# Four source blocks in one weight tile, and a new order list, in a four-layer graph network on one Trainium2 core

## The chip, the core and the metric

The kernel runs on one core of a Trainium2 chip. A core has engines that run side by side, each working through its own queue of instructions in the order in which they were written into it: TensorE for matrix products (PE in the profile; PEld is its weight load), VectorE (DVE), ScalarE (ACT), GpSimd (POOL) and SyncE (SP, which here only starts transfers). They wait for one another through semaphores. The metric is the device time of one execution in microseconds; lower is better. The time before is the median of 3 runs.

## What is computed

Sixteen graphs of 1024 nodes with 256 features each pass through four layers. Every layer normalises, applies relu, runs a graph layer and adds the result to its input. All four use the same 0/1 adjacency of their graph.

```python
h = relu(layernorm(x))
# layer 0: neighbours' mean of h @ W_msg, plus h @ W_upd + bias, relu
x = x + relu(h @ W_upd + (adj.T @ (h @ W_msg)) / deg + bias)
# layers 1 and 2: attention of 4 heads of 64 features
w = h @ W                                   # per head
alpha = softmax(where(adj, leaky(e_src[:, None] + e_dst[None, :]), -1e9))
# layer 1: relu(alpha @ w + bias) + w, layer-normed per head;  layer 2: elu(alpha @ w)
# layer 3: attention with one head of 256 features
x = x + alpha @ (h @ W3.T)
```

`adj` is 16 x 1024 x 1024, `x` is 16 x 1024 x 256, all products in float32.

## The kernel before

**Attention without a softmax pass.** The kernel uses that exp(leaky(s + d)) is a product of an exponential of each end, times the larger of two terms. For one block of 128 source nodes (`jb`, 8 blocks) one DVE instruction in `masked` (L1085) computes max(row, column) times the mask for all target nodes of a stretch. The result, a tile `p`, is the stationary operand of the products on PE. The products also sum the weights in an added column, so that dividing by it ends the softmax.

**Layers 1 and 2** (`heads`, L1235): for each of 4 heads, eight `masked` calls of 1024 targets each, and for each an 0.94 us group of products (L1266) into one accumulator `acc` in PSUM, of which there are two. `weighted` (L1285, L1286) then divides and so frees the accumulator; an epilogue follows (`epilogue1` or `epilogue2`), whose result `added` (L1218, L1229) puts on `x`: the first three heads by a transfer that accumulates, the fourth by the DVE.

**Layer 3** (`layer3`, L1396): four strips (`i2`) of 256 targets. For each strip, eight `masked` calls of 256 targets, each into a `p` tile of its own that could hold 1024 columns; for each call two float32 products, which the trace shows as four records (L1420). Then a reciprocal (L1434) and two instructions that divide and add `x` (L1445), and the transfer of the result.

**Layer 0** (`layer0`, L1094) is mostly PE work: the projection is split into two float32r parts, and the sums over neighbours (L1145, L1148) read the adjacency, which POOL's queue fetches (L884). Each layer begins with `norm_t` (L913): statistics on the DVE (L927, L934), a power on POOL (L939, L940), a shift (L946), ACT (L959), transposes on PE (L972), a copy by ACT (L978). `terms` (L1014) prepares the exponentials, checks their bounds (L1059, L1060) and sends the rows through DRAM; `spread` fetches a row `r` to all partitions (L1069).

**The order is made by a list scheduler, in Python, while the kernel is built.** Each `do(engine, cost, fn, r, w, ...)` adds an operation to a `Plan`, with an assumed cost in microseconds, the buffers that it reads and writes, and a priority (smaller is more urgent). The priority is `plan.pos` (the PE cost of all that stands before it in its graph, plus the graph's offset `b * SHIFT`, 81.5), plus a `slack`, plus a number from the table `RANK` by stage and engine. `emit` (L115) repeatedly takes the operation that could start first by its assumed times; among equals, the smaller priority. The result is a fixed order on each engine. On the chip only the true dependencies, tile by tile, hold; the assumed times do not.

**Buffers.** A tile is made when its first operation is taken from the list. `BUFS` says how many of a kind may live at once: `p` 6, `r` 3, `mask` 3, `x` 3, `acc` 2, `mm` 4. The `p` tiles are shared by all three attention layers and by the graphs in work. In the list, graph b + 2 begins after layer 3 of graph b has begun (`gates`), so two graphs are interleaved, and for a while a part of a third.

Lines spoken of: `SHIFT` L28, `RANK` L31, `do` L85, `emit` L115, `bounds` L1058, `masked` L1079, `heads` L1235, `root` L1338, `layer3` L1396, the loop over graphs L1470.

Of the kernel before, what the change touches and what calls it, by code (L numbers as in the profile page):

```python
# [19 lines left out]
P = 128  # L20
# [6 lines left out]

SHIFT = 81.5  # L28

ENGINES = ("pe", "dve", "act", "pool", "sp")  # L30
RANK = {  # L31
    "load": (-164, -252, -233, -49, -101),
    "setup": (62, -81, -47, -39, -40),
    "norm0": (-115, -341, -486, -366, -276),
    "split0": (-189, -171, -200, -288, -222),
    "mask": (426, 519, 210, 415, 404),
    "gather0": (17, -41, 92, -16, -30),
    "norm1": (-244, -92, -259, -207, -131),
    "project1": (81, 8, 5, -19, -5),
    "weights1": (-184, 20, 105, 30, 9),  # L40
    "heads1": (-93, -221, -225, -190, -118),
    "last1": (77, -76, 54, -54, 59),
    "norm2": (-121, 40, 113, 26, 32),
    "project2": (60, -110, 135, 69, 0),
    "weights2": (-27, 12, 158, -73, -4),
    "heads2": (50, -14, -243, -121, -62),
    "last2": (-122, -176, -355, -98, -89),
    "norm3": (-9, -93, -182, -62, -63),
    "project3": (301, 122, 43, 220, 174),
    "weights3": (273, 71, 138, -93, 118),  # L50
    "last3": (58, 3, 157, 80, 48),
}
# [20 lines left out]
class Plan:  # L73
# [8 lines left out]
    def __init__(self):  # L82
        self.ops, self.pos, self.gate, self.stage = [], 0.0, None, None

    def do(self, eng, cost, fn, r=(), w=(), lag=0.0, slack=0.0, kind="f", dma=0.0):  # L85

# [22 lines left out]
        bufs = list(dict.fromkeys(key[0] if isinstance(key, tuple) else key for key in (*r, *w)))  # L109
        deps.discard(k)  # L110
        self.ops.append((eng, cost, lag, fn, deps, bufs, self.pos + slack + RANK[self.stage][ENGINES.index(eng)], kind, dma))
        if eng == "pe":
            self.pos += cost

    def emit(self):  # L115
# [14 lines left out]
        while ready:  # L130
            best = None
            for k in ready:
# [9 lines left out]
                for buf in bufs:  # L142
                    if buf.t is None:
# [3 lines left out]
                        if len(ends) >= m:  # L147
# [3 lines left out]
                            at = max(at, ends[m - 1] + 0.1)  # L151
                if at is not None and (best is None or (at, prio, k) < best):
                    best = (at, prio, k)
            at, _, k = best
            eng, cost, lag, fn, deps, bufs, _, kind, dma = self.ops[k]
# [444 lines left out]
def tile_factored(  # L600
# [413 lines left out]
    def terms(wh, xw, nh, slope, ecol, scol, k):  # L1014
# [46 lines left out]

        do("dve", 0.3, bounds, r=[et, (xw, "ed")], slack=12.0)

# [14 lines left out]

    def masked(r, tt, mask, jb, h, lo, hi):  # L1079

        w = buf(work, "p", [P, N])
        do(
            "dve",
            (hi - lo + 125) / 960.0,
            lambda: nc.vector.scalar_tensor_tensor(  # L1085
                w.t[:, : hi - lo], r.t[:, lo:hi], tt.t[:, 1, h, jb : jb + 1], mask.t[:, jb, lo:hi], op0=ALU.max, op1=ALU.mult
            ),
            r=[r, (tt, 1), mask],
            w=[w],
        )  # L1090
        return w
# [143 lines left out]
    def heads(b, l, xs, mask, w, slope, epilogue, keep):  # L1235
# [15 lines left out]
        for h in range(H):  # L1251
# [23 lines left out]
            plan.stage = f"heads{l}" if h + 1 < H else f"last{l}"  # L1275
            epilogue(b, h, ps, wh, xs, 11.0 if h + 1 < H else 0.0)

# [18 lines left out]
    def epilogue1(b, h, ps, wh, xs, slack):  # L1296
# [44 lines left out]

        do("pool", 2.0, root, r=[mb], w=[rs], lag=0.9, slack=slack)
        do(
# [52 lines left out]
    def layer3(b, xs, mask):  # L1396
# [15 lines left out]
        for i2 in range(NB // 2):  # L1412
            plan.stage = "weights3"
            ps = buf(acc_p, "acc", [P, 2, 512])
            for jb in range(NB):
                w = masked(r, tt, mask, jb, 0, i2 * 2 * P, (i2 + 1) * 2 * P)

                def product(w=w, ps=ps, jb=jb):
                    for q in range(2):
                        nc.tensor.matmul(  # L1420
                            ps.t[:, q, : D + 1],
                            w.t[:, q * P : (q + 1) * P],
                            wh.t[:, jb, : D + 1],
                            start=(jb == 0),
                            stop=(jb == NB - 1),
                        )

                do("pe", 0.87, product, r=[w, (wh, jb)], w=[ps])
            k = b * NB + 2 * i2
# [11 lines left out]
            for q in range(2):  # L1441
                do(
                    "dve",
                    0.5,
                    lambda q=q, i2=i2, ps=ps, o=o, k=k: nc.vector.scalar_tensor_tensor(  # L1445
                        o.t[:, q, :],
                        ps.t[:, q, :D],
                        rdn[:, k + q : k + q + 1],
                        xs.t[:, 2 * i2 + q, :],
                        op0=ALU.mult,  # L1450
                        op1=ALU.add,
                    ),
                    r=[ps, xs],
                    w=[(o, q)],
                )
# [15 lines left out]
    for b in range(B):  # L1471
        plan.pos, plan.gate = b * SHIFT, gates.get(b)
        xs, adjr = load_x(b) if b else first, {k: load_adjr(b, k) for k in range(2)}
        mask = buf(graph, "mask", [P, NB, N], U8)
        layer0(b, xs, adjr, mask)
        heads(b, 1, xs, mask, w1c, 0.01, epilogue1, True)
        heads(b, 2, xs, mask, w2c, 0.2, epilogue2, False)
        gates[b + 2] = len(plan.ops)
        layer3(b, xs, mask)
# [76 lines left out]
```

## The time and the profile before

| | us |
|---|---|
| runs | 2736.37, 2742.13, 2742.22 |
| median | 2742.13 |
| profiled execution, its own time | 2752.51 |
| its span, first to last instruction | 2750.2 |

The profile is one execution. Busy time counts an engine's instructions, not its waits; a busy PE counts matmuls that overlap and those at a lower clock. The 40 slices each cover 68.8 us; a digit is tenths of the slice, 9 is 90% or more:

```profile
PE   7877999999999999999999999999999999999786
DVE  2699499797979979799897978979799797979984
ACT  4651745554554545545554553555545554554232
PEclk9989999999999999999999999999999999999998
```

In the middle the picture repeats every 160 to 170 us, one graph's share: slices where the DVE is at 9 (head layers) and slices where it is at 7 (layers 0 and 3). At both ends PE is at 6 to 8.

### The profile page before, as it was taken

The page shows a single profiled execution, that of the slowest core. Times are in us where ns is not written, and L with a number is a line of the kernel's source. Part 1 is how long each engine was busy: PE and PEld are TensorE (multiplying, and loading weights), DVE is VectorE, ACT ScalarE, POOL GpSimd, SP SyncE. Part 2 cuts the span into 40 slices and gives each one's busy share as a digit, 9 for nine tenths or more (in the row PEclk, how much of TensorE's full clock was granted, in tenths as well). Part 3 has the DMA queues.
Part 4 walks back from the last instruction along what each step waited for, and adds up shares of the span by engine and source line. Part 5 has one row for each costly group of instructions (what it writes and reads, how often), then busy time and mean ns, then how long its engine had stood idle before and what let it go on. Part 6 is the DMA issues. An engine that isn't in the chain of part 4 may idle for free.

```text
span 2750.2 us, 93332 instructions
## 1 busy us (share of the span) xinstructions
PE 2539.9 (92%) x40667; PEld 2265.3 (82%) x40667; DVE 2280.5 (83%) x4646; ACT 1382.1 (50%) x3777; POOL 851.7 (31%) x913
## 2 busy tenths in 40 slices
PE   7877999999999999999999999999999999999786
PEld 6766889888888888888888888888888888888675
DVE  2699499797979979799897978979799797979984
ACT  4651745554554545545554553555545554554232
POOL 3332324224242422424133242422415133241210
PEclk9989999999999999999999999999999999999998
DMA  9724647265674726556273654826657284663221
GB/s 196 172 45 92 132 89 162 51 158 84 130 111 83 165 61 140 105 117 125 57 168 72 135 102 84 163 59 139 106 101 141 48 172 76 133 101 82 34 53 28
DMA packets 397325, 293.64 MB, mean 107 GB/s; under 512 B 179301, under 2 KB 345706, under 8 KB 396906
## 3 DMA queue, kind: packets, MB, share of 16 engines
q0 software_dynamic: 232992, 92.29, 27.8%
q1 hardware_dynamic: 160752, 193.05, 24.7%
q8 instruction: 321, 5.26, 0.8%
q10 hardware_dynamic: 3162, 2.24, 0.3%
q14 instruction: 98, 0.80, 0.1%
HBM read 228.21 MB, written 17.37 MB: 89 GB/s over the span
## 4 chain that ended last, share of the span: by engine, by line
PE 39%; DVE 29%; issue 9%; POOL 8%; ACT 4%; DMA 3%; SPq 0%; POOLq 0%; DVEq 0%; ACTq 0%
DVE p L1085 12%; PE mm L989 10%; PE acc L1266 10%; PE acc L1420 9%; DVE st L927 4%; POOL rsh L1340 3%; PE mm L1184 3%; PE mm L972 3%; ACT t L1356 3%; DVE t L1369 2%; DMA x<-y 2%; DVE sth L1329 2%; DVE t L1286 2%; POOL rsh L1339 2%; DVE t L1318 1%
## 5 line engine op out<-in xcount | busy, mean ns | idle before, releaser
L1085 DVE SCALAR_TENSOR_TENSOR p<-r,et,mask 128x1024 f32<-128x1024 f32 (+1 forms) x1536 | 1471.1, 1010 | 239.2 <-PE acc L1420 179.4
L1266 PE MATMUL acc<-wide,p 128*64 128x65 f32 x32768 | 1042.8, 225 | 107.8 <-DVE p L1085 55.1
L1266 PEld LDWEIGHTS acc<-wide,p 128*64 128x64 f32 x32768 | 1001.0, 140 | 171.6 <-issue 87.8
L1420 PE MATMUL acc<-wide,p 128*128 128x257 f32 x2048 | 490.7, 394 | 59.2 <-DVE p L1085 57.9
L1420 PEld LDWEIGHTS acc<-wide,p 128*128 128x128 f32 x2048 | 393.5, 196 | 131.0 <-DVE p L1085 63.6
L989 PE MATMUL mm<-f_w,ht 128*128 128x264 f32 (+2 forms) x2048 | 476.9, 385 | 1.3 <-ACT ht L978 0.6
L989 PEld LDWEIGHTS mm<-f_w,ht 128*128 128x128 f32 x2048 | 380.2, 191 | 60.1 <-ACT ht L978 6.2
L959 ACT ACTIVATE hn<-x,shift,rstd 128x256 f32<-128x256 f32 x512 | 272.1, 592 | 239.4 <-DVE shift L946 185.7
L939 POOL TENSOR_SCALAR rstd<-mv 128x4 f32<-128x4 f32 x128 | 52.2, 407 | 763.8 <-DVE mv L934 623.9
L1356 ACT ACTIVATE t<-t,mh,rsh 128x64 f32<-128x64 f32 x512 | 176.5, 428 | 185.9 <-DVE mh L1346 161.8
L978 ACT COPY ht<-mm 128x512 f32<-128x512 f32 x256 | 144.1, 578 | 249.7 <-PE mm L972 248.8
L1145 PE MATMUL mm<-wide,adjr 128*128 128x258 f32 x1024 | 253.3, 288 | 1.6 <-DMA adjr<-in_adj_dram 1.1
L1148 PE MATMUL mm<-wide,adjr 128*128 128x256 f32 x1024 | 246.9, 282 | 0.0
L1218 POOL DMA_DIRECT2D x<-y x48 | 75.7, 1576 | 426.6 <-DVE y L1388 426.6
L1145 PEld LDWEIGHTS mm<-wide,adjr 128*128 128x128 f32 x1024 | 194.8, 190 | 3.3 <-POOL dg L1159 1.3
L1008 ACT COPY wide<-mm 128x264 f32<-128x264 f32 (+1 forms) x384 | 138.5, 378 | 114.4 <-PE mm L989 114.1
L927 DVE BATCH_NORM_STATS2 st<-x 128x6 f32<-128x256 f32 x512 | 182.5, 412 | 14.2 <-DMA x<-in_x_dram 6.6
L1148 PEld LDWEIGHTS mm<-wide,adjr 128*128 128x128 f32 x1024 | 193.1, 189 | 1.5
L972 PE MATMUL mm<-f_ident,hn 128*128 128x128 f32 x1024 | 165.8, 290 | 27.8 <-ACT hn L959 27.0
L972 PEld LDWEIGHTS mm<-f_ident,hn 128*128 128x128 f32 x1024 | 121.3, 146 | 59.5 <-ACT hn L959 39.6
L901 ACT ACTIVATE sq<-nat 128x1024 uint8<-128x1024 int32 x128 | 135.0, 1057 | 62.4 <-DMA mask<-sq 44.8
L940 POOL TENSOR_TENSOR rstd<-rstd,f_mhalf 128x4 f32<-128x4 f32 x128 | 162.8, 1272 | 10.7
(104 smaller groups left out, 2256.3 us busy)
## 6 DMA issues: line engine op xcount, KB each, us to landing
r<-rd SPq DMA_DIRECT2D x144, 512.0 KB, 3.9
adjr<-in_adj_dram POOLq DMA_DIRECT2D x128, 512.0 KB, 5.5
nat<-in_adj_dram SPq DMA_DIRECT2D x128, 512.0 KB, 6.3
out_dram<-o SPq DMA_DIRECT2D x64, 256.0 KB, 3.3
x<-in_x_dram SPq DMA_DIRECT2D x31, 512.0 KB, 4.0
x<-t POOLq DMA_DIRECT2D x48, 256.0 KB, 6.1
x<-y POOLq DMA_DIRECT2D x48, 256.0 KB, 6.0
mask<-sq SPq DMA_TRANSPOSE x128, 4.8
```

What stands on the lines that cost most here:

```text
L927: lambda st=st, ib=ib, k=k: nc.vector.bn_stats(st.t[:, k, :], xs.t[:, ib, :]),
L940: nc.gpsimd.tensor_tensor(rstd.t, rstd.t, mhalf[:, :nh], op=ALU.pow)
L959: nc.scalar.activation(hn.t[:, k, :], xs.t[:, hf * nh + q, :], AF.Relu, bias=shift.t[:, q : q + 1], scale=rstd.t[:, q : q + 1],)
L972: nc.tensor.transpose(pt.t[:, k, c, :], hn.t[:, k, c * P : (c + 1) * P], ident)
L978: nc.scalar.copy(ht.t[:, :, i0 : i0 + 2 * P].rearrange("p c (k i) -> p k c i", k=2), pt.t)
L989: nc.tensor.matmul(out, ht.t[:, c, ib * P : (ib + 1) * P], w.t[:, c, lo:hi], start=(c == 0 and k == 0), stop=(c == KC - 1), skip_group_che ...
L1085: lambda: nc.vector.scalar_tensor_tensor(w.t[:, : hi - lo], r.t[:, lo:hi], tt.t[:, 1, h, jb : jb + 1], mask.t[:, jb, lo:hi], op0=ALU.max, ...
L1145: nc.tensor.matmul(ps.t[:, : D + 2], a.t[:, ib, :], hi.t[:, ib, : D + 2], start=(ib == 0), stop=False)
L1148: nc.tensor.matmul(ps.t[:, :D], a.t[:, ib, :], lo.t[:, ib, :D], start=False, stop=(ib == NB - 1))
L1266: nc.tensor.matmul(ps.t[c : c + 64, g, q * E1 : (q + 1) * E1], p.t[:, i2 * 64 : (i2 + 1) * 64], xw.t[:, jb, h * E1 : (h + 1) * E1], start= ...
L1356: nc.scalar.activation(t.t[:, ib, :], t.t[:, ib, :], AF.Identity, bias=mb.t[:, 3, ib : ib + 1], scale=rs.t[:, ib : ib + 1],)
L1420: nc.tensor.matmul(ps.t[:, q, : D + 1], w.t[:, q * P : (q + 1) * P], wh.t[:, jb, : D + 1], start=(jb == 0), stop=(jb == NB - 1),)
```

## The change

Six things change, all in the way the list is made, one of them also in the tiles.

1. In layer 3, four consecutive source blocks write their 256 columns side by side into one `p` tile of 1024. The next tile begins with the next four. The products read their quarter. Quarters have dependencies of their own in the list (`(w, q)`).
2. All `masked` operations of one graph are chained in the list, each after the one before (`row="weights"`).
3. `emit` holds: having found the operation that could start first, it looks among those of the same engine that could start within `HOLD` (PE 0.12, DVE 0.15, ACT 0.35 us, POOL and SP 0) and takes the most urgent one.
4. Each graph gets an offset of its own, `b * 95.75 + START[b]`, in place of `b * 81.5`.
5. All of `RANK` is new.
6. Some assumed costs and slacks change: the bound check, the per-head root, layer 3's output, the slack of the head epilogues (11 to 104) and of the bound check (12 to 89.143).

```diff
-SHIFT = 81.5
+SHIFT = 95.75
 ENGINES = ("pe", "dve", "act", "pool", "sp")
+HOLD = (0.12, 0.15, 0.35, 0.0, 0.0)
+START = (130, 200, 204, 145, 92, 50, 26, 28, -26, -33, -47, -83, -83, -117, -100, -132)
 RANK = {
...
-    "gather0": (17, -41, 92, -16, -30),
+    "gather0": (235, 22, 55, -72, -11),
...
-    "weights1": (-184, 20, 105, 30, 9),
-    "heads1": (-93, -221, -225, -190, -118),
+    "weights1": (-34, 128, 52, 210, 144),
+    "heads1": (37, -149, -193, 13, -83),
...
-    "weights2": (-27, 12, 158, -73, -4),
-    "heads2": (50, -14, -243, -121, -62),
+    "weights2": (148, 81, 209, -47, 55),
+    "heads2": (-244, -14, -294, 42, -9),
...
-    "norm3": (-9, -93, -182, -62, -63),
-    "project3": (301, 122, 43, 220, 174),
-    "weights3": (273, 71, 138, -93, 118),
-    "last3": (58, 3, 157, 80, 48),
+    "norm3": (-470, -404, -342, -391, -261),
+    "project3": (197, 283, 166, -88, -39),
+    "weights3": (3, 273, 28, -2, 7),
+    "last3": (-257, -439, -291, -314, -293),
 }
...
         deps.discard(k)
+        if row is not None:
+            if row in self.rows:
+                deps.add(self.rows[row])
+            self.rows[row] = k
...
-            best = None
+            best, could = None, []
...
-                if at is not None and (best is None or (at, prio, k) < best):
-                    best = (at, prio, k)
-            at, _, k = best
+                if at is not None:
+                    could.append((at, prio, k))
+                    if best is None or could[-1] < best:
+                        best = could[-1]
+            at, prio, k = best
+            until = at + HOLD[ENGINES.index(self.ops[k][0])]
+            for a, p, q in could:
+                if self.ops[q][0] == self.ops[k][0] and a <= until and p < prio:
+                    at, prio, k = a, p, q
...
-        do("dve", 0.3, bounds, r=[et, (xw, "ed")], slack=12.0)
+        do("dve", 0.45, bounds, r=[et, (xw, "ed")], slack=89.143)
...
-    def masked(r, tt, mask, jb, h, lo, hi):
-        w = buf(work, "p", [P, N])
+    def masked(r, tt, mask, jb, h, lo, hi, w=None, q=0):
+        w = w or buf(work, "p", [P, N])
+        c = q * (hi - lo)
         do(
             "dve",
             (hi - lo + 125) / 960.0,
             lambda: nc.vector.scalar_tensor_tensor(
-                w.t[:, : hi - lo], r.t[:, lo:hi], tt.t[:, 1, h, jb : jb + 1], mask.t[:, jb, lo:hi], op0=ALU.max, op1=ALU.mult
+                w.t[:, c : c + hi - lo],
...
-            w=[w],
+            w=[(w, q)],
+            row="weights",
         )
...
-            epilogue(b, h, ps, wh, xs, 11.0 if h + 1 < H else 0.0)
+            epilogue(b, h, ps, wh, xs, 104.0 if h + 1 < H else 0.0)
...
-        do("pool", 2.0, root, r=[mb], w=[rs], lag=0.9, slack=slack)
+        do("pool", 2.6, root, r=[mb], w=[rs], lag=1.2, slack=slack)
...
             for jb in range(NB):
-                w = masked(r, tt, mask, jb, 0, i2 * 2 * P, (i2 + 1) * 2 * P)
-                def product(w=w, ps=ps, jb=jb):
-                    for q in range(2):
+                q = jb % 4
+                w = masked(r, tt, mask, jb, 0, i2 * 2 * P, (i2 + 1) * 2 * P, w if q else None, q)
+                def product(w=w, ps=ps, jb=jb, q=q):
+                    for k in range(2):
+                        c = (2 * q + k) * P
                         nc.tensor.matmul(
-                            ps.t[:, q, : D + 1],
-                            w.t[:, q * P : (q + 1) * P],
+                            ps.t[:, k, : D + 1],
+                            w.t[:, c : c + P],
...
-                do("pe", 0.87, product, r=[w, (wh, jb)], w=[ps])
+                do("pe", 0.87, product, r=[(w, q), (wh, jb)], w=[ps])
...
-                    0.5,
+                    0.43,
...
     for b in range(B):
-        plan.pos, plan.gate = b * SHIFT, gates.get(b)
+        plan.rows = {}
+        plan.pos, plan.gate = b * SHIFT + START[b], gates.get(b)
```

More of the change, by code (lines that the diff above doesn't have):

```diff
@@ L26 @@
 TERM_MAX = 30.0
-SHIFT = 81.5
+SHIFT = 95.75
 ENGINES = ("pe", "dve", "act", "pool", "sp")
+HOLD = (0.12, 0.15, 0.35, 0.0, 0.0)
+START = (130, 200, 204, 145, 92, 50, 26, 28, -26, -33, -47, -83, -83, -117, -100, -132)
 RANK = {
[L32 to L36, printed above, removed]
-    "gather0": (17, -41, 92, -16, -30),
-    "norm1": (-244, -92, -259, -207, -131),
-    "project1": (81, 8, 5, -19, -5),
-    "weights1": (-184, 20, 105, 30, 9),
-    "heads1": (-93, -221, -225, -190, -118),
-    "last1": (77, -76, 54, -54, 59),
-    "norm2": (-121, 40, 113, 26, 32),
-    "project2": (60, -110, 135, 69, 0),
-    "weights2": (-27, 12, 158, -73, -4),
-    "heads2": (50, -14, -243, -121, -62),
-    "last2": (-122, -176, -355, -98, -89),
-    "norm3": (-9, -93, -182, -62, -63),
-    "project3": (301, 122, 43, 220, 174),
-    "weights3": (273, 71, 138, -93, 118),
-    "last3": (58, 3, 157, 80, 48),
+    "load": (-503, -236, -325, -519, -331),
+    "setup": (208, 175, -147, -87, 84),
+    "norm0": (11, -271, -21, -82, -102),
+    "split0": (-150, -231, -259, -383, -298),
+    "mask": (-51, 325, -17, 224, 245),
+    "gather0": (235, 22, 55, -72, -11),
+    "norm1": (-27, 10, -299, -56, -103),
+    "project1": (-20, 58, -51, -176, -4),
+    "weights1": (-34, 128, 52, 210, 144),
+    "heads1": (37, -149, -193, 13, -83),
+    "last1": (-30, -37, -199, -390, -78),
+    "norm2": (-258, -107, 30, 143, -53),
+    "project2": (-260, -306, -495, -57, -204),
+    "weights2": (148, 81, 209, -47, 55),
+    "heads2": (-244, -14, -294, 42, -9),
+    "last2": (160, -1, -30, -7, 1),
+    "norm3": (-470, -404, -342, -391, -261),
+    "project3": (197, 283, 166, -88, -39),
+    "weights3": (3, 273, 28, -2, 7),
+    "last3": (-257, -439, -291, -314, -293),
 }
@@ L82, in __init__, with do @@
     def __init__(self):
-        self.ops, self.pos, self.gate, self.stage = [], 0.0, None, None
-    def do(self, eng, cost, fn, r=(), w=(), lag=0.0, slack=0.0, kind="f", dma=0.0):
+        self.ops, self.pos, self.gate, self.stage, self.rows = [], 0.0, None, None, {}
+    def do(self, eng, cost, fn, r=(), w=(), lag=0.0, slack=0.0, kind="f", dma=0.0, row=None):
         k, deps = len(self.ops), set() if self.gate is None else {self.gate}
@@ L1085, in masked @@
             lambda: nc.vector.scalar_tensor_tensor(
-                w.t[:, : hi - lo], r.t[:, lo:hi], tt.t[:, 1, h, jb : jb + 1], mask.t[:, jb, lo:hi], op0=ALU.max, op1=ALU.mult
+                w.t[:, c : c + hi - lo],
+                r.t[:, lo:hi],
+                tt.t[:, 1, h, jb : jb + 1],
+                mask.t[:, jb, lo:hi],
+                op0=ALU.max,
+                op1=ALU.mult,
             ),
             r=[r, (tt, 1), mask],
-            w=[w],
+            w=[(w, q)],
+            row="weights",
         )
```

## The prediction

> **What bounds the kernel now.** I began with the page: busy shares, the 40 slices, the chain. Then busy time in four stretches, then the waits of PE and DVE inside those stretches, and last the timeline where one wait repeats.
>
> ```profile
> PE 2539.9 (92%) x40667; PEld 2265.3 (82%) x40667; DVE 2280.5 (83%) x4646; ACT 1382.1 (50%) x3777; POOL 851.7 (31%) x913
> PE 39%; DVE 29%; issue 9%; POOL 8%; ACT 4%; DMA 3%; SPq 0%; POOLq 0%; DVEq 0%; ACTq 0%
> ```
>
> PE is busy 92% of the span and DVE 83%; the chain that ended last changes between them. No single engine is a wall for the whole run: what is left is 2750.2 − 2539.9 = 210 us in which PE does nothing. Where these lie (columns: stretch, its length, busy time and instructions of PE, PEld, DVE, ACT, POOL, granted clock, DMA share, GB/s):
>
> ```profile
> 0.00:100.00 100.00, 80.73 (x501) 71.25 (x502) 26.59 (x104) 53.90 (x135) 36.05 (x77) 1.00 0.90 192
> 100.00:300.00 200.00, 154.66 (x3292) 140.69 (x3291) 179.18 (x341) 91.64 (x253) 66.35 (x50) 0.91 0.42 84
> 300.00:2550.00 2250.00, 2152.17 (x34527) 1919.79 (x34528) 1933.74 (x3911) 1184.65 (x3248) 721.14 (x764) 0.99 0.56 111
> 2550.00:2750.00 200.00, 152.38 (x2352) 133.56 (x2350) 140.97 (x290) 51.91 (x143) 28.19 (x22) 0.91 0.19 39
> ```
>
> Four parts: 19 us at the load, 45 us between 100 and 300 (DVE 90% busy, PE 77%: the first two graphs are both in the head layers, nothing else is there for PE), 98 us in the long middle (4.3% of it), 48 us at the end, when the last graph runs alone. What PE waits for in the middle, and what DVE waits for (columns: total us, times, longest):
>
> ```profile
> PE acc L1420 <- DVE p L1085: 47.9, 38, 3.6
> PE acc L1266 <- DVE t L1286: 20.2, 14, 1.6
> PE acc L1266 <- issue: 9.7, 10, 2.3
> PE acc L1266 <- DVE p L1085: 9.7, 23, 0.5
> ...
> DVE p L1085 <- PE acc L1420: 159.2, 60, 9.2
> ```
>
> The reader is to see a pair. Layer 3's products (L1420) are late by 47.9 us in total because the DVE has not written their weights; yet the DVE stood still 159.2 us, in the same 2250 us, because it could not get a tile to write layer 3's weights into. Both cannot be a lack of DVE speed. By durations PE is the slower partner in layer 3:
>
> ```profile
> L1085 DVE SCALAR_TENSOR_TENSOR p<-r,et,mask 128x1024 f32<-128x1024 f32 x1024 | 1251.3, 1277 | 42.2 <-PE acc L1266 28.1 <-PE acc L1420 10.4 <-DMA r<-rd 3.4
> L1420 PE MATMUL acc<-wide,p 128*128 128x257 f32 x2048 | 490.7, 394 | 59.2 <-DVE p L1085 57.9 <-issue 1.3
> L1085 DVE SCALAR_TENSOR_TENSOR p<-r,et,mask 128x256 f32<-128x256 f32 x512 | 223.1, 476 | 197.0 <-PE acc L1420 169.0 <-DMA r<-rd 15.0 <-PE acc L1266 9.8
> ```
>
> A block of layer 3 costs the DVE 0.476 us. On PE it is four matmul records, and the chain's pieces of L1420 (24 in 5.20 us) give 0.217 each, 0.87 us a block. Six tiles ahead is 6 × 0.476 = 2.9 us of DVE work; then the DVE, which takes its instructions in order, stops, and when it is sent to a head layer's weights (1.277 us each), a norm or an epilogue of the other graph, PE soon has nothing of layer 3. The timeline shows both; around 1056:
>
> ```profile
> 1054.11 0.36 DVE L934 BATCH_NORM_AGGREGATE mv<-st 128x2 f32<-128x6 f32 x4
> 1054.39 1.37 DVE L927 BATCH_NORM_STATS2 st<-x 128x6 f32<-128x256 f32 x4
> ...
> 1056.33 2.07 DVE L1085 SCALAR_TENSOR_TENSOR p<-r,et,mask 128x256 f32<-128x256 f32 x3
> ...
> 1056.86 2.89 PE L1420 MATMUL acc<-wide,p 128*128 128x257 f32 x8 [1.87 <-DVE p L1085]
> ```
>
> [...] Here the granted clock is 0.91 in both stretches where PE starves and 0.99 in the middle, so starving costs a little twice. [...] 1277 and 476 ns for 1024 and 256 columns are 1.04 ns a column plus 209 ns. The change keeps 256 columns, so nothing of that is saved.
>
> **The change part by part.** Against the profiled execution's span, 2750.2 us (its time, 2752.5, is 10.4 above the median shown, 2742.1; I take a difference in span as the same difference in the median).
>
> (a) Work: no matmul, DVE instruction or DMA is added, removed or resized. The products read as many columns as before, and holds, row edges and offsets exist only while the list is made. 0 us. All else is order and waiting.
>
> (b) Four source blocks in one tile. A layer 3 strip needs 2 tiles, not 8; six tiles hold up to 24 blocks, 11.4 us of DVE work, 21 us of PE work. The DVE can write these in the stretch where it now stands and PE is the bound (33 to 35 us busy of 50 at 1100 to 1160), and then turn to the other graph while PE lives on the stock. Target: the 47.9 us. Bounds: 0 (the six tiles are shared, and heads of the other graph take them) and −48; plus as much as 10 us from the end, where PE also waited 10.0 us so. A wait of up to 3.6 us is covered by 5 blocks in stock, so most should go; but late next is the product's accumulator (two PSUM buffers) or another producer. I take two thirds of 47.9, −30. A claimed tile is held from its first quarter's write to its fourth product, at least 4 × 0.87 = 3.5 us; that is the price in the slower rival's neighbourhood, hidden as long as five other tiles suffice for heads that use one each 1.3 us.
>
> (c) Head epilogues later (slack 11 to 104), the holds, and truer costs. A hold lets DVE wait 0.15 us and PE 0.12 us for a more urgent instruction: the normalise that frees an accumulator (L1286), which PE awaited 20.2 us in 14 places, can go ahead of a 1.277 us weight. Bounds: −20, and + the holds themselves: some 30 changes of work a graph × 16 × 0.12 = +58 if PE held at each, which only happens if nothing is gained. ACT's 0.35 us hold is hidden: it is 50% busy. The new costs are nearer the trace: the bound check measures 0.213 + 0.201 = 0.41 (was 0.3, now 0.45), layer 3's output 0.47, or 0.84 to 0.88 a pair (was 0.5, now 0.43), the root 0.94 + 2.36 = 3.3 (was 2.0 + 0.9 lag, now 2.6 + 1.2). A list that believes truer times should stall less. I take −8.
>
> (d) Weights in order: all of a graph's weights had one priority by stage and rising positions, so mostly in order already. The new edge makes one late row copy hold back that graph's later weights; behind it in the DVE's queue stand only later heads. The waits for the row copy are 18.4 us in 4 places over the run. 0, bounds ±10.
>
> (e) Offsets and ranks. Start: graph 1 was 81.5 behind graph 0 in the priority count, now 95.75 + 200 − 130 = 165.75. The DVE works for graph 0 first, so graph 0 reaches layer 3, and graph 2's gathers may start, earlier. Of the 128 head-layer weights of two graphs some 97 were done in 100 to 300. Of the 45 us idle there 33 lie between 150 and 270, when the last norm of graph 0 ran (120 us, PE busy 87.0). I take about half of these: −15, bounds 0 and −35. End: the last gap falls from 81.5 to 95.75 − 132 + 100 = 63.75, so graph 15 is closer behind graph 14 and its lone tail (48 us idle in 200) shorter: −10, bounds +10 and −30. Middle: the graph periods, read off the repeats of one layer 3 run in the chain, go from 161 to 168 us, 164 on the mean; the new offsets may reach the best everywhere (12 × 2 = −24) or miss. Their gain is already in (b) and (c): 0, bounds −24 and +30.
>
> In (e), SP's and POOL's transfers move with their graphs; DMA is 56% busy in the middle and no transfer stands high among PE's waits, so 0 is taken.
>
> Sum: −30 − 8 − 15 − 10 = −63. Span 2750 − 63 = 2687; median 2742 − 63 = 2679, rounded to 2680.
>
> **The rivals.**
>
> 1. Stock doesn't help: PE finds the next late thing at once, since in the middle it is 95.7% busy anyway; only start and end gain. For it: waits move readily when both engines are near full (DVE 86% there). Against it: DVE's 159 us idle are real room. −15 to −25: about 2720.
>
> 2. The list also closes gaps inside what counts as busy. L1266 at 30.3 ns a record (128 in 3.88 us) would need 993 us, its row has 1042.8; L1420 at 217 ns 444, its row has 490.7: 96 us of stretch, part from the low clock. Half of that on top: −63 − 48, about 2630.
>
> 3. Slower: graphs fall in step. The offsets now make gaps of 36.5, 43, 53.75 and 41.75 among graphs 2 to 7 where all were 81.5. If neighbours so spaced do their head layers together, the middle gets stretches like 100 to 270: between 150 and 250 PE did 71.4 of 100 us, against 95.7% in the middle, so 100 us in step costs 24 us. It decides beyond 63 / 0.24 = 260 us in step, that is, more than about 65 us for each of the four gaps. At 370 us: +89 − 63 = +26, 2768. For it: it is seen at the start. Against it: each instruction takes whatever can start first and graph b + 2 waits for graph b's layer 3, which pulled the old list into half-step by 300 us.
>
> 4. It does not do what it says: quarters of one tile are tracked as a whole, so that the next quarter's write waits for the product of the last. Then 384 of 512 blocks would alternate, 0.48 us of idle PE each unless filled: up to +184. Against it: scaling head h + 1's columns of the wide tile (L1247 at 1041.40) runs while the products of head h read other columns of it, and doesn't wait. 3 in 100, counted as slower.
>
> **How the numbers follow.** Forecast (−35 to −90) 0.46; rival 1 (−6 to −35) 0.18; rival 2 (beyond −90) 0.14; no change, the gains and (c), (d) cancelling, 0.05; rival 3 0.14; rival 4 0.03. Faster 0.78, same 0.05, slower 0.17; 0.2% (5.5 us) is about what a measurement of this kernel can tell. The forecast's own range is 2652 to 2707. For 8 in 10 I go down to 2625 for most of rival 2, and up to 2755, which takes in rival 1, no change and the nearest part of rival 3.
>
> **What would show it.** Right: "DVE p waits for PE acc L1420" falls well under 100 us and "PE acc L1420 waits for DVE p" under 20 in the middle; PE over 80% in 100 to 300; a period near 161. Step (b) is wrong if these waits fall and PE's idle time in the middle stays near 98 us under other names. (e) is wrong if the first 300 us still hold 60 us of idle PE. Rival 3 shows as new slices with clock under 0.95 and DVE at 9 in the middle. The prediction falls if DVE's waits for p move to L1266, heads starved of tiles.

## The result: slower, 2836.32 us

| | before | after |
|---|---|---|
| median | 2742.18 | 2836.32 |
| runs from, to | 2736.37 to 2745.86 | 2828.93 to 2838.81 |
| span of the profiled execution | 2750.2 | 2835.9 |
| PE busy | 2539.9 | 2566.4 |

The ratio is 1.034, with a 95% interval of 1.031 to 1.037: 94 us lost where 63 were forecast as a gain. In the two profiled spans the loss is 85.7 us, and it has two parts: PE is busy 26.5 us longer with the same 40667 instructions, and it stands still 59.2 us longer. The page of the kernel after, its line of busy shares and three of its rows of 40 slices (70.9 us each):

```profile
PE 2566.4 (90%) x40667; PEld 2288.9 (81%) x40667; DVE 2273.4 (80%) x4646; ACT 1391.4 (49%) x3777; POOL 911.0 (32%) x913
PE   6868999989899898989989899898989989899786
DVE  2569888787897979788787997878789787897973
PEclk9979999999999999999999999999999999999898
```

Before, PE stood at 9 in every slice of the middle. Now an 8 comes back every two or three slices, about once per graph. The DVE, too, is busy a smaller share. The stretches in the order of those shown of before (length; busy time and instructions of PE, PEld, DVE, ACT, POOL; granted clock; DMA share; GB/s):

```profile
0.00:100.00 100.00, 77.02 (x447) 66.32 (x448) 25.28 (x97) 51.51 (x118) 33.08 (x72) 0.98 0.99 196
100.00:300.00 200.00, 148.79 (x2955) 132.49 (x2954) 159.33 (x299) 88.70 (x251) 54.05 (x49) 0.89 0.43 86
300.00:2550.00 2250.00, 2101.94 (x33579) 1879.01 (x33578) 1881.41 (x3856) 1154.24 (x3136) 776.16 (x753) 0.98 0.59 108
2550.00:2830.00 280.00, 238.65 (x3692) 211.04 (x3689) 207.36 (x397) 96.99 (x276) 47.73 (x39) 0.93 0.22 47
```

In the middle PE stands still for 2250 − 2101.94 = 148 us (before 98). In the first 300 us it is 74 (before 65). So the start did not gain, and most of the loss lies in the stretch that repeats.

The start of layer 3's first product in each graph dates the graphs: 306.0 for the first and 2438.6 for the fourteenth before, 320.9 and 2523.6 after. That divides the 85.7 us of span: 14.9 before the first of these; 2202.7 − 2132.6 = 70.1 in the thirteen periods (164.0 us each before, 169.4 after); 0.7 behind. **The loss is 5.4 us per graph.**

The waits of PE and DVE in the middle, the same stretch as before (total us, times, longest):

```profile
PE acc L1288 <- DVE p L1101: 58.7, 13, 7.6
PE acc L1288 <- issue: 45.2, 25, 4.2
PE acc L1444 <- DVE p L1101: 17.9, 20, 2.1
...
DVE f_mx L1073 <- ACT et L1067: 86.8, 13, 6.7
DVE f_rdn L1458 <- PE acc L1444: 51.4, 13, 4.0
DVE p L1101 <- DMA r<-rd: 47.9, 15, 4.9
...
DVE p L1101 <- PE acc L1444: 20.5, 13, 1.6
```

L1288 is the heads' product (L1266 before), L1444 layer 3's (L1420), L1101 the masked weights. The pair that the prediction aimed at has fallen: the DVE's wait for layer 3's products from 159.2 to 20.5 us, theirs for the DVE from 47.9 to 17.9. The 20.5 us that are left belong to weights of the heads, not of layer 3. But the DVE now waits elsewhere: at the bound check (`f_mx`) for ACT, at layer 3's reciprocal (`f_rdn`) for its products, and for the row copy. And the heads' products, which had waited 9.7 us for their weights from the DVE, now wait 58.7, about once per graph.

**Where in a period.** One period of each kernel, in windows of 40 us that start with layer 3. First everything, then PE's records of layer 3's product line alone. Before:

```profile
1287.00:1327.00 40.00, 40.00 (x226) 35.23 (x225) 25.18 (x80) 24.08 (x77) 12.98 (x21) 1.00 0.36 76
1327.00:1367.00 40.00, 38.34 (x861) 34.65 (x861) 38.44 (x45) 17.09 (x51) 6.28 (x4) 1.00 0.26 42
1367.00:1407.00 40.00, 36.40 (x643) 32.36 (x641) 35.54 (x78) 18.62 (x48) 9.55 (x12) 0.96 0.75 167
```

```profile
1287.00:1327.00 40.00, 17.40 (x79) 14.46 (x78) 1.00 0.36 76
1327.00:1367.00 40.00, 2.23 (x11) 1.61 (x9) 1.00 0.26 42
1367.00:1407.00 40.00, 10.26 (x40) 7.97 (x40) 0.96 0.75 167
```

After:

```profile
1336.00:1376.00 40.00, 38.88 (x208) 33.78 (x207) 26.68 (x84) 21.05 (x67) 12.08 (x16) 1.00 0.62 90
1376.00:1416.00 40.00, 39.71 (x702) 35.83 (x703) 37.25 (x56) 10.59 (x26) 12.66 (x11) 1.00 0.18 60
1416.00:1456.00 40.00, 32.30 (x770) 30.04 (x769) 33.55 (x52) 20.34 (x60) 10.20 (x9) 0.91 0.77 142
```

```profile
1336.00:1376.00 40.00, 21.46 (x96) 17.62 (x94) 1.00 0.62 90
1376.00:1416.00 40.00, 7.09 (x32) 6.00 (x32) 1.00 0.18 60
1416.00:1456.00 40.00, 0.00 (x0) 0.00 (x0) 0.91 0.77 142
```

Before, 10.26 us of layer 3's products stand in the third window, 80 us behind the first one, in the midst of head layers, where the DVE is busy 35.54 of the 40 us. After, nothing of layer 3 is left there, and PE does 32.30 of 40 us at a clock of 0.91. From its first record to its last, one graph's layer 3 took 101.6 us before and 52.1 us after (medians over the sixteen graphs). The timeline of PE in that third window:

```profile
1428.00 3.95 PE L1288 MATMUL acc<-wide,p 128*64 128x65 f32 x128 [0.38 <-issue]
1433.67 3.90 PE L1288 MATMUL acc<-wide,p 128*64 128x65 f32 x127 [1.71 <-issue]
1440.72 4.09 PE L1288 MATMUL acc<-wide,p 128*64 128x65 f32 x85 [3.15 <-issue]
1447.26 3.63 PE L1288 MATMUL acc<-wide,p 128*64 128x65 f32 x64 [2.46 <-DVE p L1101]
```

and of the DVE beside it:

```profile
1437.23 2.47 DVE L1101 SCALAR_TENSOR_TENSOR p<-r,et,mask 128x1024 f32<-128x1024 f32 x2
1439.62 0.68 DVE L1410 SCALAR_TENSOR_TENSOR y<-y,t 128x512 f32<-128x512 f32 x1
1440.33 0.69 DVE L1251 TENSOR_TENSOR x<-x,y 128x512 f32<-128x512 f32 x1
1442.70 1.41 DVE L941 BATCH_NORM_STATS2 st<-x 128x6 f32<-128x256 f32 x4 [1.68 <-DMA x<-y]
...
1445.87 2.45 DVE L1101 SCALAR_TENSOR_TENSOR p<-r,et,mask 128x1024 f32<-128x1024 f32 x2
```

Here PE has head products alone. The DVE makes two weights, then an epilogue and the next layer's statistics, and no other weight for six microseconds. PE runs dry each time: what stands behind in its queue is more of the heads' products and, from 1450.8 us on, the next norm's transposes.

### The profile page after: what moved, and what is told of

Read it like the earlier page. It is cut to its first block, busy times and chain, and to the rows that moved or that the text cites. A ratio compares the mean times of both kernels' runs of the same rounds, so it can differ in the third digit from the quotient of the medians.

```text
span 2835.9 us, 93167 instructions
## 1 busy us (share of the span) xinstructions
PE 2566.4 (90%) x40667; PEld 2288.9 (81%) x40667; DVE 2273.4 (80%) x4646; ACT 1391.4 (49%) x3777; POOL 911.0 (32%) x913
## 5 line engine op out<-in xcount | busy, mean ns | idle before, releaser
L1101 DVE SCALAR_TENSOR_TENSOR p<-r,et,mask 128x1024 f32<-128x1024 f32 (+1 forms) x1536 | 1466.4, 1009 | 113.7 <-DMA r<-rd 66.4
L1288 PE MATMUL acc<-wide,p 128*64 128x65 f32 x32768 | 1084.3, 228 | 171.3 <-DVE p L1101 95.6
L1288 PEld LDWEIGHTS acc<-wide,p 128*64 128x64 f32 x32768 | 1031.4, 142 | 253.0 <-issue 188.4
L1003 PE MATMUL mm<-f_w,ht 128*128 128x264 f32 (+2 forms) x2048 | 486.0, 388 | 24.4 <-ACT ht L992 24.3
L1444 PE MATMUL acc<-wide,p 128*128 128x257 f32 x2048 | 463.4, 383 | 25.7 <-DVE p L1101 25.5
L1444 PEld LDWEIGHTS acc<-wide,p 128*128 128x128 f32 x2048 | 385.4, 191 | 86.8 <-DVE p L1101 14.8
L953 POOL TENSOR_SCALAR rstd<-mv 128x4 f32<-128x4 f32 x128 | 79.7, 622 | 885.6 <-DVE mv L948 857.3
L954 POOL TENSOR_TENSOR rstd<-rstd,f_mhalf 128x4 f32<-128x4 f32 x128 | 191.5, 1496 | 10.7
L1188 ACT ACTIVATE o<-mm,dg 128x256 f32<-128x256 f32 x128 | 58.6, 469 | 269.8 <-POOL dg L1182 151.5
L986 PE MATMUL mm<-f_ident,hn 128*128 128x128 f32 x1024 | 163.0, 291 | 16.4 <-ACT hn L973 12.0
```

What stands on the lines that cost most here:

```text
L954: nc.gpsimd.tensor_tensor(rstd.t, rstd.t, mhalf[:, :nh], op=ALU.pow)
L986: nc.tensor.transpose(pt.t[:, k, c, :], hn.t[:, k, c * P : (c + 1) * P], ident)
L1003: nc.tensor.matmul(out, ht.t[:, c, ib * P : (ib + 1) * P], w.t[:, c, lo:hi], start=(c == 0 and k == 0), stop=(c == KC - 1), skip_group_che ...
L1101: lambda: nc.vector.scalar_tensor_tensor(w.t[:, c : c + hi - lo], r.t[:, lo:hi], tt.t[:, 1, h, jb : jb + 1], mask.t[:, jb, lo:hi], op0=ALU ...
L1288: nc.tensor.matmul(ps.t[c : c + 64, g, q * E1 : (q + 1) * E1], p.t[:, i2 * 64 : (i2 + 1) * 64], xw.t[:, jb, h * E1 : (h + 1) * E1], start= ...
L1444: nc.tensor.matmul(ps.t[:, k, : D + 1], w.t[:, c : c + P], wh.t[:, jb, : D + 1], start=(jb == 0), stop=(jb == NB - 1),)
```

## The experiments

What was to be told apart. **A, the order:** the new list runs layer 3 at once, packed and beside the next graph's gathers, where PE has too much and the DVE too little; the head layers then lack PE work that needs little of the DVE. The new numbers of the list (ranks, offsets, holds, slacks) do this, not the tile. **B, the tile:** a tile with four blocks is held until its last block's product, and the heads lack tiles. **C, the bound check:** in the new order it stands first in the DVE's queue and waits for ACT, and everything behind it is late. **D** is the dose of B: a cost that grows with the number of blocks in a tile. **E, the holds:** they make an engine stand.

Six of the kernels carry one edit against before or after; the other three have a list searched anew. "List's end" is the end that `emit` returns by its own assumed costs (the old costs in before and runs 1, 4 and 5, the new ones in the others); "layer 3" is the median time from a graph's first to its last product record of layer 3; the period is the mean of the ten from the second to the twelfth graph's first product of layer 3. The ratio is to the runs of before on the same chip.

| run | us | ratio to before, 95% | list's end | layer 3 | period |
|---|---|---|---|---|---|
| before | 2742.18 | | 2657.0 | 101.6 | 164.4 |
| after | 2836.32 | 1.031 to 1.037 | 2705.2 | 52.1 | 169.5 |
| old order, four in a tile | 2787.90 | 1.014 to 1.019 | 2657.0 | 104.9 | 166.7 |
| old order, two in a tile | 2742.98 | 0.996 to 0.998 | 2657.0 | 101.3 | 163.0 |
| after, check moved | 2836.14 | 1.032 to 1.037 | 2705.2 | 52.2 | 168.8 |
| after, last strip late | 2799.42 | 1.017 to 1.023 | 2707 | 97.8 | 166.5 |
| before, last strip early | 2832.99 | 1.031 to 1.035 | 2765 | 52.8 | 171.1 |
| after, no holds | 2859.58 | 1.038 to 1.042 | 2781 | 47.4 | 171.3 |
| new list, four in a tile | 2724.63 | 0.989 to 0.993 | 2642 | 98.4 | 160.5 |
| new list, one in a tile | 2707.82 | 0.983 to 0.987 | 2654 | 94.7 | 159.6 |
| the same order, two in a tile | 2708.68 | 0.984 to 0.988 | 2653.6 | 94.6 | 159.8 |

**1. The tile alone.** Before's list, instruction for instruction; only where layer 3's weights lie is new. Six tiles, as before.

```diff
+    def quarter(group):
+        def make():
+            if not group:
...
+                group.append(work.tile([P, N], F32, tag="p", name=f"p_{count[0]}", bufs=P_TILES))
+            return group[0]
+        return Buf("p", make)
...
-                w = masked(r, tt, mask, jb, 0, i2 * 2 * P, (i2 + 1) * 2 * P)
+                q = jb % 4
+                if not q:
+                    group = []
+                w = masked(r, tt, mask, jb, 0, i2 * 2 * P, (i2 + 1) * 2 * P, quarter(group), q)
```

> The list of before, instruction for instruction on all five engines; only layer 3's weights of four source blocks lie in one tile, as in the change. Theory A (the new list costs the 94 us, the tile does not): at most before, 2715 to 2745 us; the DVE's wait for layer 3's products falls below 100 us from 179. Rival B (the shared tile costs: slots held until the fourth product, or quarters waiting for each other): 2790 us or more, with new DVE waits for PE at the weights.

2787.90 us, against 2744.09 of before on the same chip. The waits in 300 to 2550:

```profile
DVE f_mx L1062 <- ACT et L1056: 130.4, 14, 10.4
DVE p L1098 <- PE acc L1279: 79.9, 74, 3.6
...
PE acc L1279 <- DVE t L1299: 43.0, 13, 3.4
...
PE acc L1279 <- DVE p L1098: 24.6, 22, 1.6
```

The wait that the change aimed at is gone altogether, and 130.4 us are now spent at the bound check, the next instruction in the DVE's queue that can't start. So the 159.2 us were not room that the old order could use. And the tile itself costs here. The DVE's rows for the heads' weights, in 300 to 2550, of before, of this run and of the kernel after, end with the idle time before them:

```profile
L1085 DVE SCALAR_TENSOR_TENSOR p<-r,et,mask 128x1024 f32<-128x1024 f32 x872 | 1065.5, 1277 | 35.6 <-PE acc L1266 24.9 <-PE acc L1420 10.4
L1098 DVE SCALAR_TENSOR_TENSOR p<-r,et,mask 128x1024 f32<-128x1024 f32 x854 | 1049.7, 1278 | 82.4 <-PE acc L1279 79.9 <-DMA r<-rd 0.9
L1101 DVE SCALAR_TENSOR_TENSOR p<-r,et,mask 128x1024 f32<-128x1024 f32 x841 | 1034.1, 1275 | 46.6 <-PE acc L1288 24.7 <-PE acc L1444 20.5 <-DMA r<-rd 1.2
```

They wait 79.9 us for a tile, where it was 35.3 before (24.9 and 10.4). A was wrong on this run; B was right in direction, 2 us short of its range: +44 us. That is under the old order, though, and half of the loss. In the kernel after the same wait is 45.2 us (24.7 and 20.5), 10 more than before, so the price of this run isn't seen there at its full size.

**2. The bound check moved.** In the kernel after, the check is emitted behind the first masked weights of its layer.

```diff
-            fn()
+            if fn.__name__ == "bounds" and bufs[0] not in begun:
+                late[bufs[0]] = fn
+            else:
+                fn()
+                if fn.__name__ == "weigh_p":
+                    begun.add(bufs[1])
+                    late.pop(bufs[1], lambda: None)()
```

> The kernel after with each bound check moved on the DVE behind the first weights of its layer, the rest of the order the same. Rival C (a bound check that is listed too early blocks the DVE for 135 us in all while it waits for ACT, and the heads are late because of that): 2760 to 2800 us. Theory A (the DVE has nothing else to do at that point of the list): the wait goes to the next instruction, the row copy, and the time stays at 2826 to 2840 us.

2836.14 us: nothing. The DVE's two largest waits in 300 to 2550:

```profile
DVE f_rdn L1468 <- PE acc L1454: 144.8, 13, 11.1
DVE p L1106 <- DMA r<-rd: 42.4, 14, 4.6
```

The 86.8 us that the check had waited stand at the reciprocal now (51.4 before the edit). The wait moved, as A had said, but to the reciprocal, not to the row copy (42.4 us, 47.9 before the edit). The name of a wait says where the queue stood, not what it cost. C falls.

**3. Layer 3's last strip later, in the kernel after.** The fourth strip's weights and products get a slack of 300, so that they are left for the head layers.

```diff
+LAST = 300.0
...
-                w = masked(r, tt, mask, jb, 0, i2 * 2 * P, (i2 + 1) * 2 * P, w if q else None, q)
+                w = masked(r, tt, mask, jb, 0, i2 * 2 * P, (i2 + 1) * 2 * P, w if q else None, q, LAST if i2 == 3 else 0.0)
...
-                do("pe", 0.87, product, r=[(w, q), (wh, jb)], w=[ps])
+                do("pe", 0.87, product, r=[(w, q), (wh, jb)], w=[ps], slack=LAST if i2 == 3 else 0.0)
```

> The kernel after, but the last of layer 3's four strips gets a slack of 300, so that it stays as filler for PE while the other graph is in its head layers: the list spreads one graph's layer 3 products over some 96 us where the kernel after has 52 (before 102). Form A1 of theory A (layer 3 packed together with the next graph's gathers leaves PE without filler in the head layers): faster than after by 40 us or more, 2750 to 2795. Form A2 (the list is worse for other reasons too, its period in its own assumed times stays 161 us a graph): 2825 to 2850 us.

2799.42 us: 37 of the 94 us are back, with nothing but the fourth strip's urgency changed and a list that by its own costs is 2 us longer. That is A1's direction, a little short of its 40 us, and far from A2. Layer 3 spreads over 97.8 us, the period falls from 169.5 to 166.5. PE's idle time in 300 to 2550 is back where it was: 94 us, against 148 in the kernel after and 98 before. What remains of the loss is almost all busy time: PE is busy 2581.2 us here and 2539.9 before, 41 of the 46 us between the two spans.

**4. Layer 3's last strip earlier, in the kernel before.** The mirror image, in the old list with a tile for each block: the same edit with `LAST = -150.0`.

> The kernel before, but with a slack of -150 on the last strip of layer 3, one number: the list then packs one graph's layer 3 into some 52 us. Theory A: slower than before by 80 us or more, about 2850, with PE idle before the heads' products and no shared tile in it. Rival B (tile): the tile is the old one, so 2742 and no more than 20 us away.

2832.99 us, +89 on before: a loss as large as the change's, without its tile and without its numbers. Layer 3 takes 52.8 us there, as in the kernel after. PE's largest wait in the middle:

```profile
PE acc L1269 <- DVE shift L948: 110.2, 12, 13.9
```

It is again the heads' product that stands, once per graph, 110.2 us. It waits for another DVE instruction than in the kernel after; what is the same is that behind it in PE's queue stand more of the heads' products and the next norm's transposes, and nothing of layer 3. The loss is not a copy of the change's. PE is busy 2540.8 us, as before, so that all of it is idle time; the periods swing between 140 and 196 us, where those of after keep to 168 to 172; and this list ends 108 us later by its own costs.

**5. Two blocks in a tile.** As the first, with `q = jb % 2`.

> As e1, the list of before instruction for instruction, but two source blocks share a tile, not four. Theory D (what e1 cost is the holding of slots: a shared tile is free only after the last product of its blocks): between before and e1, 2755 to 2775 us, with less DVE waiting for the heads' products than e1's 83 us. Rival (a fixed cost of sharing, such as quarters tracked as one tile): as e1, 2780 to 2795 us.

2742.98 us, ratio 0.997: no slower than before, where four cost 44 us, and below both expectations. The heads' weights wait 32.0 us for a tile, not 79.9. So sharing has no fixed cost, and the tiles' waits fit D's account, the time for which a slot is held; but the cost does not grow in proportion: two blocks cost nothing, four do. The DVE stands at the bound check here too (121.7 us), at no loss.

**6 and 7. Two lists searched anew.** `RANK`, `HOLD` and the graphs' offsets were searched anew for the shortest list by its own costs, in both cases with the slack of the epilogues and of the bound check at their old 11 and 12. The sixth keeps the change's other parts, four blocks in a tile among them; the seventh has one block in a tile and no chain of weights. Against the kernel after, of the seventh:

```diff
-SHIFT = 95.75
-HOLD = (0.12, 0.15, 0.35, 0.0, 0.0)
-START = (130, 200, 204, 145, 92, 50, 26, 28, -26, -33, -47, -83, -83, -117, -100, -132)
+HOLD = (0.0, 0.031626, 0.549667, 0.0, 0.0)
+START = (489.97174, 642.885086, 119.709984, 423.63007, 463.840796, 695.328505, 707.082586, 917.829828, 824.842651, 497.504513, 593.353611, 863.95061, 748.720999, 625.501664, 789.573893, 1137.144655)
...
-    "weights3": (3, 273, 28, -2, 7),
-    "last3": (-257, -439, -291, -314, -293),
+    "weights3": (4889, 3806, 1039, 510, -3319),
+    "last3": (1100, -161, -1217, -725, -1259),
...
-            row="weights",
...
-                q = jb % 4
+                q = 0
```

> The changed kernel's form (four blocks in a tile, holds, chained weights, its costs) with the two old slacks (12 and 11) and other numbers in RANK, HOLD and the offsets, for which the list by its own assumed times ends at 2642 us; before ends at 2657, after at 2705. Theory A (the numbers of the list cost the time): 2720 to 2755 us. Rival B (the shared tile costs whatever the list is): 2780 us or more.

> The same search, but each block of layer 3 in a tile of its own as in before, no chain of weights; holds and the new costs kept. Its list ends at 2654 us by its own assumed times. If time goes with the list's own end: 2730 to 2765 us, some 10 us over e6. If the shared tile costs: 25 us or more under e6.

2724.63 us for the sixth, ratio 0.991: with four blocks in a tile it is faster than before, and 112 us faster than after. So four blocks in a tile do not force the loss: with other numbers in the list (the two old slacks among them) it is gone. 2707.82 us for the seventh, the fastest of all, ratio 0.985. In both, layer 3 spreads over 95 to 98 us. The seventh beats the sixth by 17 us though its list is 12 us longer. So here time does not go with the list's own end, and the gap, which is the sharing's direction, is less than the 25 us that had been named for it. The two lists differ in their numbers too, so it can't be put down to the tile.

**8. No holds.** The kernel after with `HOLD` at −1 for each engine, so that none is made.

> The kernel after without holds, all else kept, so that the list is made anew: it ends at 2781 us by its own assumed times, where after ends at 2705. Rival E (holds let engines stand idle and cost the time): faster than after, 2780 to 2820. Theory A: slower than after, 2860 to 2920 us.

2859.58 us, 23 more than after, or 15 by the ratios, since this chip's runs of before are slower too; A's range began at 2860. The holds help this list; E falls. Its list ends 76 us later by its own costs, so less than a third of that is seen.

**9. The good order with two in a tile.** The seventh's list, unchanged, with two blocks of layer 3 in a tile as in the fifth.

> The instruction order of the e7 list (one tile per block, 2707.82 us), unchanged, but two consecutive blocks of a layer 3 strip share one tile of the six, as in e5. Theory A (the time is set by which instruction stands where; the tile changes only how long a slot is held and how often the DVE stops for one): with two blocks a slot is held for about one more block, which the six tiles bear, so within 10 us of 2708 (2698 to 2718), with the DVE's waits for layer 3's products lower than in e7 and as much of its idle time under other names. Rival B (a shared tile is the gain that the change wanted, and a good list can use it): below 2695. Rival D (sharing costs in any list, by slots held): above 2720.

2708.68 us against 2707.82: the same. The DVE's largest wait in 300 to 2550 in the seventh, then the ninth, where a weight's wait for layer 3's products is 0.6 us:

```profile
DVE p L1100 <- PE acc L1442: 133.9, 57, 8.4
```

```profile
DVE f_mx L1075 <- ACT et L1069: 115.3, 16, 9.1
```

This is what A had expected. The fastest kernel has the very wait that the change removed, 133.9 us of it, and taking it away puts 115.3 us at the bound check and leaves the time as it was.

**Not measured.** Four blocks in a tile in the seventh's order, where with six tiles the engines would wait for one another in a circle; the change's numbers with one block in a tile, for which `emit` comes to a point where nothing that is left can start, so that the tile's share in the change's own order has no number; and each of the new ranks, offsets and slacks alone.

## Why the prediction was wrong

**(a) The work, 0 us: right in counts, not in PE's time.** All instruction counts are equal, but PE is busy 26.5 us longer. The heads' product line is the largest part:

```profile
L1288 PE MATMUL acc<-wide,p 128*64 128x65 f32 x32768 | 1084.3, 228 | 171.3 <-DVE p L1101 95.6 <-issue 45.2 <-ACT y L1404 9.1
```

It was 1042.8 before. The prediction had used the lower clock of starved stretches in its second rival, as a possible gain; in part it came as a loss. In the kernel after, the granted clock is 0.91 in the window 1416 to 1456, where PE is busy 81%, and 0.83 in its second half, where it is busy 72%. By the trace's clock records PE worked at half the clock for 91 us before and for 122 after. Half of the difference, 15 us, is an estimate of the clock's part in the 26.5; it assumes that work at half the clock lasts twice as long, which it nearly did (after, 64 of the heads' products took 3.63 us at a clock of 0.52, 57 ns each, and 128 took 3.95 at 1.00, 31 each). The clock isn't all: run 3 has 94 us at half the clock (its mean clock is 0.974, that of before 0.978) and is busy 41 us longer than before, and run 6, with the highest mean clock of all (0.985), has 1069.9 us in its heads' products. What goes along with the rest is how often PE changes between the heads' products and other work: 354 times before, 502 after, 638 in run 6, 662 in run 3, and 354 to 392 in the other lists. In every trace other work starts a median of 152 or 153 ns after the start of a record of the heads' products, where the next of these products starts after some 30 on the mean. Without holds (run 8) it is 390 changes, so PE's hold seems to make many of them. No run changes this alone, so it is argued, not shown.

**(b) Four blocks in one tile, −30 us: the waits went, the gain did not come.** Both named waits fell below the marks that the prediction had set, and its own test for "(b) is wrong" came true: PE's idle time in the middle did not fall below 98 us; it is 148, under other names. The flaw is the sentence that both waits can't be a lack of DVE speed, so that the DVE's 159.2 us "are real room". Behind the stalled weight in the DVE's queue stood a bound check that could not start either: with the weight's wait gone, the DVE stood 130.4, 121.7 and 115.3 us there (runs 1, 5 and 9). PE's 47.9 us did fall by 30, the very size forecast, but PE's waits at the heads' product (the rows of the two views of waits summed) went from 39.6 to 114.0. The price of holding a tile, put at nothing "as long as five other tiles suffice", is 44 us under the old order with four blocks, and nothing with two (runs 1 and 5). The want of a free tile was the cause of the DVE's gap: in run 1 the tile alone took the 159.2 us away. But where layer 3 begins (1287 to 1327, before) the engine with no room is PE, busy 40.00 of 40 us, and not the DVE with its 25.18; giving the DVE room moved the gap and gained no time. What counted was the place of layer 3: a quarter of it moved into the heads' stretch returned 37 us (run 3), and moved out of it cost 89 (run 4).

**(c) Slack, holds, costs, −8 us: the sign of the holds right.** Without them the kernel is 15 to 23 us slower. The slack of 104 and the truer costs weren't tried one by one, since each makes another list.

**(d) Weights in order, 0 us: right.** Without the chain, the change's list gives the same order of instructions on all five engines.

**(e) Offsets and ranks: the step that failed.** Start −15, measured +14.9; PE's idle time in the first 300 us is 74, above the mark of 60. End −10, measured +0.7. And "Middle: ... Their gain is already in (b) and (c): 0", with bounds of −24 and +30: the middle as a whole came out at +70, thirteen times 5.4, where (b), (c) and this term were to make −38. Among the numbers in the diff stood a sign of it: in `weights3` PE's went from 273 to 3, in `weights1` and `weights2`, which hold the heads' products, from −184 to −34 and from −27 to 148, and the whole of `norm3` and `last3` to between −470 and −257. Read as positions, these make layer 3's products 270 more urgent for PE and the heads' 150 and 175 less, where neighbouring graphs are 78 apart on the mean (95.75 − 262 / 15). (The DVE's number for layer 3's weights went the other way, from 71 to 273, so the numbers alone don't settle it.) The prediction looked at the offsets between graphs, which are one term of the priority, and took `RANK`, the larger one, at no effect. What came in place of the 0 is layer 3 packed into 52 us and PE idle in the head layers: in 300 to 2550 its idle time went from 98 to 148 us, and run 3, which moves a quarter of layer 3 back, has 94. Runs 3 and 4 move the priority of one strip of layer 3 and of nothing else, by 300 later and 150 earlier: −37 and +89 us. And a part of the loss could be read before any run, from the end that `emit` returns while the kernel is built: priced at the same new assumed costs, the old order ends at 2684.7 us and the new one at 2705.2.

**The rivals.** The picture of the third came in part: a stretch of head layers with PE starved at a clock of 0.91, though with the DVE at 84%, not 90%. Its cause was another. The graphs did not fall in step (the first thirteen distances between them are 168 to 172 us); what PE could have done beside the heads had been done already. (Its gaps are a little off: 36.75, 42.75 and 53.75 lie between graphs 2 and 5, and the 41.75 between 7 and 8.) The first and second rivals ended on the wrong side. The fourth is refuted by the 17.9 us that layer 3's products wait.

**What is shown and what is open.** Shown: a list with four blocks in a tile can be faster than before (run 6); packing layer 3 makes a loss of this size in the old list (run 4); spreading one strip returns 37 us and with them nearly all the idle time that PE had gained in the middle (run 3). Open: the other 55 us between run 3 and before on its chip, 2744.09, nearly all of it PE's longer busy time.

The list's ends tell a part. The new list ends 48 us later than the old one, but 28 of these come with the new assumed costs; at equal costs the new order is 20.5 us longer, in run 3 22, and which of the hundred numbers makes that isn't known. The other 74 us of the change's 94 no list foresaw. Priced at the new costs, the chip's times lie 43 to 58 us above the lists' ends in the five kernels with one or two blocks in a tile (before, runs 4, 5, 7 and 9) and 78 to 131 us in the six with four (after, runs 1, 2, 3, 6 and 8). That speaks for a share of B in the loss, beyond what the heads' waits for a tile show. It is not shown, since the orders differ as well; in run 3, for one, the heads' weights wait 63.8 us for a tile, and run 3 with two blocks in a tile wasn't measured. Run 4, with a tile for each block, loses 89 us where its list had foreseen 105. Some of the difference shows in waits that assumed costs can't see: 47.9 us for the row copy after, 11.5 in run 7, 3.7 in run 3.

## What to carry to other kernels

A long wait is room only if something behind it in the same queue could have run; in runs 1 and 9 nothing could, and 130.4 and 115.3 us turned up at the bound check behind it. Freeze the order, take the wait away, and see where the idle time turns up, before a gain is booked. Ask too which engine is the limit where the wait stands. Cut one period into windows and ask of each which engine is short and what filler it has; work that is light on the limiting engine, like layer 3's last strip here, was worth more late in the scarce stretch than early in the rich one (37 us back in run 3, 89 lost in run 4). When a planner's numbers change, look first at the end of its own plan, with both orders priced at the same costs, and work out which stage they move past which; a tile changed beside them may gain nothing.

## What the runs showed of the hardware

In the kernel after, PE's granted clock stood at half for a while behind two pauses (0.50 from 1447.5 to 1450.5). In the timeline of the third window, 128 of the heads' products take 3.95 us at the full clock. Behind a pause of 3.15 us, 85 take 4.09, and behind one of 2.46 us, 64 take 3.63; the windows around these three groups (columns as above; the clock is the third number from the end):

```profile
1428.00:1431.90 3.90, 3.90 (x128) 3.81 (x128) 3.90 (x5) 3.72 (x13) 0.00 (x0) 1.00 0.79 246
1440.70:1444.80 4.10, 4.08 (x85) 3.95 (x84) 2.42 (x11) 0.00 (x0) 0.24 (x2) 0.62 1.71 238
1447.30:1450.80 3.50, 3.50 (x64) 3.46 (x64) 3.50 (x6) 2.08 (x4) 2.84 (x2) 0.52 0.03 5
```

Behind the pause of 1.71 us, between the first two groups of that timeline, the clock was not lower: 1.00 from 1433.67 to 1437.57, and the 127 products there took 3.90 us.

POOL's power for the norm, the same 128 instructions, took a median of 1047 ns before, 1048 in run 7, but 1459 after; its first half (the addition before it) 228, 247 and 492 ns. The distributions of the kernel after, line by line (duration in ns, least, median, greatest):

```profile
L953 POOL TENSOR_SCALAR rstd<-mv x128: 224/492/1205, 7.6 to 2776.9; 128x4 f32<-128x4 f32 x128
L954 POOL TENSOR_TENSOR rstd<-rstd,f_mhalf x128: 1031/1459/1987, 7.9 to 2777.2; 128x4 f32<-128x4 f32 x128
```

The least values are those of before (222 and 1032), so the same instruction is stretched at some times and not at others; by what wasn't settled. The DVE's wait for it is 24.2 us in the middle, against 1.3 before; but it is 15.6 in run 7 too, so the stretch isn't all of that. The list counts 1.35 us for the pair in both kernels, which fits before (1.28 by the medians) and not after (1.95).
